# Attention's norms brought to the features' partitions by block transposes and DRAM instead of TensorE transposes

## Chip, cores and metric

The kernel runs on one core of one Trainium2 chip. The metric is the device time of one execution in microseconds (us). A core has TensorE (PE in the profile: matmuls, and transposes as matmuls against an identity; PEld is its weight load), VectorE (DVE), ScalarE (ACT), GpSimd (POOL) and SyncE (SP), which here only issues DMAs. Each engine works through its own instructions in order, and waits for the others by semaphores. SBUF is the memory on the chip, with 128 partitions; PSUM holds what TensorE writes; DRAM lies outside.

## What is computed

Four sequences of 512 tokens with 256 features go through a gated-scan attention and then six FFN blocks, all in f32:

```python
# x: (4, 512, 256)
x = x + layernorm(attn(layernorm(x)))
x = x + layernorm(ffn(layernorm(x)))

# attn(x), hidden sizes 128 and 512
q = silu(x @ Wq1 @ Wq2);  f = sigmoid(x @ Wk1 @ Wk2);  v = x @ Wv
a = sigmoid(f)                          # exp(log_sigmoid(f))
h[t] = a[t] * h[t - 1] + (1 - a[t]) * v[t]      # along the tokens
out = q * h
attn = (out * rsqrt(mean(out * out) + 1e-6) * norm_w) @ Wo

# ffn(x): six blocks, hidden size 1024
for i in range(6):
    x = gelu(x @ W1[i].T + B1[i]) @ W2[i].T + B2[i] + x
    if i < 5: x = layernorm(x) * LN_G[i] + LN_B[i]
```

Each sequence has two norms in front of matmuls that concern this case: the *first norm*, ahead of the attention, and the *second norm*, ahead of the FFN. A layernorm is taken over the features of one token, so it is done with tokens on the partitions; the matmuls that follow sum over features, so they want features on the partitions. Between the two the data has to be transposed.

## The kernel before

**Layout.** A sequence's x lies as four tiles of 128 tokens by 256 features (`xs[b][t]`). `token_stats` (L658) and `rstd_of` (L668) make a norm's mean and reciprocal deviation on DVE and POOL, and `normalized` (L682) applies them on ACT into a tile of the ring `nns` (named n in the profile).

**To the features, first way.** `to_features` (L699) takes the four normalized tiles and, for each half d of the features, lets TensorE transpose four blocks of 128x128 into one PSUM tile (`pt`), which ACT copies to SBUF (128x512). Attention's first norms (`Attention.features`, L774, and `first_features`, L779) and second norms (`ffn_input`, L896) go this way.

**To the features, second way.** `passage` (L733) takes the same tiles through DRAM. DVE transposes every 32x32 block in two instructions of 128x512 (`blocks_transposed`, L712); SP stores the result to a DRAM tile of the ring `passed` (512 KB); `collected` (L722) reads it back in four DMAs of 128 KB, each to 32 partitions, so that blocks come to lie in the right partitions; then ACT copies each half d while it puts the columns in order (four tiles by four groups by 32 columns). The norms between FFN blocks go this way (`Norm.norm`, L1148, and `Norm.features`, L1191), where that last copy also applies the scale and the bias. A passage takes two buffers of `rooms` (the four x tiles, and two `room` tiles that attention's output projection uses), gives one back at once and the other after the copies.

**Order of work.** The Python code only records operations, with a cost and with the buffers that they read and write, slice by slice. `Plan.run` (L302) then simulates the engines and writes out each engine's instructions: of those that can start it takes the one that is due first (`Plan.latest`, L285: backward from the end of TensorE's work). So a change in one place moves instructions elsewhere. The semaphores are put in afterwards from what each instruction reads and writes. All stores and nearly all loads are issued by SP, in that written order.

**Stages.** Sequences go through attention one after another (the loop at L1235). While sequence b is in its projections and scans, the first norm of b+1 is prepared, the output projection of b-1 is done (`output`, L853; `residual`, L868, which makes x1 = x + layernorm(attention) and the statistics of the second norm), and the second norm of b-2 is brought to the features (`ffn_input`). Each scan takes sigmoids on ACT, the scan on DVE, and products and sums on POOL. The FFN works on two sequences at a time (g = 0 is sequences 0 and 1): `input_sums` (L649) makes 18 sums of input blocks (`tx`, B_SUMS) on POOL, `w1_sums` 19 sums of weight blocks (`sa`), and `Hidden` multiplies these and the plain blocks, in a scheme with fewer products; `Output` does the second matmul. The second norms of sequences 2 and 3 come to the features while the FFN's first half (i = 0, g = 0) runs; this is ordered by class `Attended` (L1208).

Buffers that matter: `txs` are 18 tiles of 128x256; the first four serve as features of sequence 0, and the last as the source of warm-up matmuls; the others lie idle until the first `input_sums`. `xts[g][d][n]` hold the features that enter the FFN (xt in the profile), `tcs` the features of attention (tc).

Of the kernel before, what the change touches and what calls it, by code (L numbers as in the profile page):

```python
# [12 lines left out]
AF = mybir.ActivationFunctionType  # L13
# [3 lines left out]
P = 128  # L17
# [123 lines left out]
def lines_of(text):  # L141
    return [line.split() for line in text.strip().split("\n")]
# [205 lines left out]
def kernel(  # L348
# [46 lines left out]
    def tiles(name, shape, n=1, pool=sb):  # L395
        return [
            Buf(pool.tile(shape, F32, tag=f"{name}{k}", name=f"{name}_{k}"))
            for k in range(n)
        ]
# [39 lines left out]
    w2_s = tile_of("w2", [P, NH, E])  # L439
    sa = tiles("sa", [P, 2 * P], len(lines_of(A_SUMS)))  # L440
    sb2 = tiles("sb", [P, NP, P], 4)
    txs = tiles("tx", [P, 2 * P], len(lines_of(B_SUMS)))

    wide = Pool(tiles("tmp", [P, S], 14))

# [12 lines left out]
        [View((v, *xs[b]), v.ap, (0,) * (NT + 1)) for b, v in enumerate(x_of)]  # L458
        + [View((v, *ys.bufs[2 * k : 2 * k + 2]), v.ap, (0,) * 3) for k, v in enumerate(roomy)]
    )  # L460
    passed = Ring(tiles("passed", [P, NT * E], 4, dram))
    banks = Pool(tiles("bank", [P, S], 6, ps))
    pts = Ring(tiles("pt", [P, S], 2, ps))
    sts = Ring(tiles("st", [P, 6], 6))
# [5 lines left out]
    def act(dst, src, func=AF.Copy, bias=None, scale=None):  # L470
        given = [(k, p) for k, p in (("bias", bias), ("scale", scale)) if p is not None]
        ptrs = [p for _, p in given if isinstance(p, View)]
        kw = {k: p.ap if isinstance(p, View) else p for k, p in given}
        plan.op(
            "ACT",
            0.054 + 0.00084 * src.size + 0.11 * len(ptrs),
            lambda: nc.scalar.activation(dst.ap, src.ap, func, **kw)  # L477
            if func != AF.Copy
            else nc.scalar.copy(dst.ap, src.ap),  # L479
            [src, *ptrs],  # L480
            [dst],
        )
# [153 lines left out]
    def x_blocks(g):  # L636

        blocks = {
            f"b{k}{c}": xts[g][k][c // 2][:, ts(c % 2, 2 * P)]
            for k in range(ND)  # L640
            for c in range(4)
        }
        blocks.update((f"t{n}", t) for n, t in enumerate(txs))
        return blocks

    def w1_sums(i):
# [35 lines left out]
    def normalized(src, by, t):  # L682

        r, nb = by
        z = nns.next()
        to = z
        if len(src.ap.shape) == 3:
            to = z.with_ap(z.ap.rearrange("p (f r) -> p f r", r=src.ap.shape[2]))
        act(to, src, AF.Identity, nb[:, t : t + 1], r[:, t : t + 1])
        return z  # L690
# [8 lines left out]
    def to_features(srcs, d, xt, scale=None, bias=None):  # L699


        pt = pts.next()[:, : len(srcs) * P]
        for t, src in enumerate(srcs):
            transpose(pt[:, ts(t, P)], src[:, ts(d, P)])
        if scale is None:
            act(xt, pt)
        else:
            act(xt, pt, AF.Identity, bias, scale)
# [21 lines left out]

        plan.op("SP", 0.45 * Q, emit, [there], [to], to.size * P * 4 / 0.26e6)

    def passage(tokens):  # L733

        block, there, to = rooms.next(), passed.next(), rooms.next()
        by_pair = block.with_ap(block.ap.rearrange("p (f t c) -> p f t c", t=NT, c=32))
        for k in range(0, NT, 2):
            z = tokens[k : k + 2]  # L740
            pair = pairs[id(z[0].bufs[0])].rearrange("p (t f r) -> p f t r", t=2, r=32)
            blocks_transposed(by_pair[:, :, k : k + 2, :], pair, *z)
        store(there, block)
        collected(there, to)
        rooms.back(block)
        return to

    class Attention:

# [4 lines left out]
        def norm(self):  # L754
            self.n, mv = [], mvs.next()
            for t in range(NT):
                token_stats(mv, xs[self.b][t], t)
            by = rstd_of(mv, rs.next())
            for t in range(NT):
                self.n.append(normalized(xs[self.b][t], by, t))  # L760
            self.xt = []

        def first_norm(self):
            self.n = []
# [8 lines left out]

        def features(self, d):  # L774
            xt = tcs.next()
            to_features(self.n, d, xt)
            self.xt.append([xt])

        def first_features(self, half):  # L779

# [87 lines left out]
        def residual(self):  # L868
# [24 lines left out]
                store(kept[self.b][t], x1)  # L893
            self.x1_by = rstd_of(mv1, rs.next())

        def ffn_input(self, d):  # L896

            if d == 0:
                self.n1 = [normalized(xs[self.b][t], self.x1_by, t) for t in range(NT)]
            g, n = divmod(self.b, 2)  # L900
            to_features(self.n1, d, xts[g][d][n])

    class Row:

# [236 lines left out]
    class Norm:  # L1141
# [6 lines left out]
        def norm(self, n):  # L1148

            room, mv = self.output.tokens[n], mvs.next()  # L1150
            by_tile = room.ap.rearrange("p (f t r) -> p t f r", t=NT, r=32)
            y = [room.with_ap(by_tile[:, t]) for t in range(NT)]
            for t in range(NT):
                token_stats(mv, y[t], t)
            by, tokens = rstd_of(mv, rs.next()), []
            for t in range(NT):
                z = normalized(y[t], by, t)
                tokens.append(z)
                if self.i == NB - 1:
                    b = 2 * self.g + n  # L1160
                    tt("POOL", z, z, self.x[n][:, ts(t, E)], ALU.add)
                    store(out[b, ts(t, P), :], z)
            rooms.back(room)
            if self.i < NB - 1:
                self.there[n] = passage(tokens)
            else:
                rooms.back(self.x[n])

# [22 lines left out]
        def features(self, u):  # L1191
            if self.i == NB - 1:
                return
            n, d = divmod(u, ND)
            src, dst = self.there[n][:, ts(d, S)], xts[self.g][d][n]
            act(
                dst.with_ap(dst.ap.rearrange("p (t g c) -> p g t c", t=NT, g=Q)),
                src.with_ap(src.ap.rearrange("p (g t c) -> p g t c", t=NT, g=Q)),
                AF.Identity,
                be_s[:, self.i, d : d + 1],  # L1200
                g_s[:, self.i, d : d + 1],
            )
            if d == ND - 1:
                rooms.back(self.there[n])
            if u == 2 * ND - 1:
                input_sums(self.g)

    class Attended:  # L1208
# [8 lines left out]
        def norm(self, u):  # L1217
            if u == 0:
                self.both[1].residual()

        def features(self, u):
            n, d = divmod(u, ND)
# [12 lines left out]
    for b in range(B):  # L1235
        one = att[b]
        past = att[b - 1] if b else None
        one.k1_q1()
        if b == 0:
            for _ in range(FILL):  # L1240
                plan.op("PE", 0.43, lambda: warm(P), [one.n[1]], [unread])
        if b + 1 < B:
            att[b + 1].norm()
        one.value(0)
        one.scan(0)
        one.value(1)
        if past:
            past.output(0)
        one.scan(1)
        if past:  # L1250
            past.output(1)
        one.value(2)
        if past:
            past.output(2)
        one.scan(2)
        if past:
            past.output(3)
        one.value(3)
        if past:
            past.residual()  # L1260
        if b >= 2:
            att[b - 2].ffn_input(0)
        if b + 1 < B:
            att[b + 1].features(0)
        one.scan(3)
        if b >= 2:
            att[b - 2].ffn_input(1)
        if b + 1 < B:
            att[b + 1].features(1)
# [3 lines left out]
    w2_sums()  # L1273

    output, norm = None, Attended(att[2], att[3])
    for i in range(NB):
        for g in range(NG):
            last, hidden = output, Hidden(i, g)
            if last:
                hidden.take(HEAD)  # L1280
                while last.left:
                    last.take(BY[0])
                    hidden.take(BY[1])
                norm = Norm(*of, last)
            else:
                hidden.take(4)
            if g == 0:
                if i:
                    load_w2(i)
                    w2_sums()  # L1290
                if i + 1 < NB:
                    load_w1(i + 1)
            if last:
                for n in range(2):
                    hidden.take(2)
                    if of[0] == NB - 1:
                        norm.load_x(n)
                    norm.norm(n)
            else:
                for u in range(4):  # L1300
                    hidden.take(2)
                    norm.tokens(u)
                norm.norm(0)
            hidden.take(26)
            if g == 1 and i + 1 < NB:
                w1_sums(i + 1)
            output = Output(i, g, hidden)
            for u in range(4):
                output.take(2)
                norm.features(u)  # L1310
            output.take(len(output.left) - DEFER)
            of = (i, g)
# [57 lines left out]
```

## Time and profile before

| | |
|---|---|
| times of three runs | 693.93, 694.00, 694.45 us (median 694.0) |
| profiled execution | 694.03 us, of which the profile's span is 691.4 us |
| granted TensorE clock, mean | 0.996 |
| transposes of `to_features` on PE | 64, between 6.2 and 145.3 us |
| attention, by PE's first and last instruction of it | about 6 to 123 us |
| DVE block transposes | 84, all between 144 and 636 us |
| DMA | 67.4 MB in 74,444 packets, mean 98 GB/s |

The span is what the profiler covers; the execution's time has some 2.6 us around it. In the profile's group rows, "x64 | 10.1, 283 | 0.0" says: 64 instructions, 10.1 us busy in all, 283 ns mean of one, and the idle time of the engine just before them with what ended it. An f32 matmul of the kernel shows as two matmul records, a transpose as one. The view of waits lists per engine: who waited for whom, us in total, times, longest. Timeline rows give the start, the length, the engine, the line and what was written from what, with equal neighbours merged. Here are the engines' shares of the attention and the first FFN half, from the view by windows (us busy):

| window | PE | DVE | ACT | POOL | DMA share |
|---|---|---|---|---|---|
| 15 to 45 | 30.0 | 16.4 | 20.2 | 28.5 | 0.24 |
| 45 to 75 | 30.0 | 19.7 | 20.0 | 22.0 | 0.06 |
| 75 to 105 | 30.0 | 14.7 | 19.5 | 20.7 | 0.05 |
| 105 to 135 | 29.6 | 19.9 | 21.4 | 27.1 | 0.20 |
| 135 to 165 | 30.0 | 14.9 | 11.9 | 22.4 | 0.09 |

### The profile page before, as it was taken

The page shows a single profiled execution, that of the slowest core. Times are in us where ns is not written, and L with a number is a line of the kernel's source. Part 1 is how long each engine was busy: PE and PEld are TensorE (multiplying, and loading weights), DVE is VectorE, ACT ScalarE, POOL GpSimd, SP SyncE. Part 2 cuts the span into 40 slices and gives each one's busy share as a digit, 9 for nine tenths or more (in the row PEclk, how much of TensorE's full clock was granted, in tenths as well). Part 3 has the DMA queues.
Part 4 walks back from the last instruction along what each step waited for, and adds up shares of the span by engine and source line. Part 5 has one row for each costly group of instructions (what it writes and reads, how often), then busy time and mean ns, then how long its engine had stood idle before and what let it go on. Part 6 is the DMA issues. An engine that isn't in the chain of part 4 may idle for free.

```text
span 691.4 us, 8158 instructions
## 1 busy us (share of the span) xinstructions
PE 677.8 (98%) x2376; PEld 440.9 (64%) x2376; DVE 460.2 (67%) x885; ACT 358.2 (52%) x625; POOL 528.6 (76%) x688
## 2 busy tenths in 40 slices
PE   9999999999999999999999999999999999999994
PEld 7565568856747658568476475584674765855853
DVE  5566455745956948839659569487495694793955
ACT  3847756842724635536447346354473482463732
POOL 4997659694978758986679887589866798865862
PEclk9999999999999999999999999999999999999998
DMA  8300002102254042351341541414514305316411
GB/s 252 100 1 31 27 4 90 33 16 89 79 153 152 31 148 66 148 169 48 119 126 63 167 136 46 150 49 166 169 30 148 96 1 194 110 61 182 138 46 62
DMA packets 74444, 67.43 MB, mean 98 GB/s; under 512 B 5792, under 2 KB 64160, under 8 KB 74400
## 3 DMA queue, kind: packets, MB, share of 16 engines
q1 hardware_dynamic: 73568, 65.99, 29.8%
q10 hardware_dynamic: 832, 0.92, 0.4%
q8 instruction: 19, 0.31, 0.2%
q14 instruction: 25, 0.20, 0.1%
HBM read 40.68 MB, written 26.21 MB: 97 GB/s over the span
## 4 chain that ended last, share of the span: by engine, by line
PE 71%; DVE 14%; POOL 6%; ACT 4%; issue 3%; DMA 1%; DVEq 0%; ACTq 0%; POOLq 0%
PE bank L526 66%; DVE ht L494 8%; POOL tc L494 5%; PE pt L526 4%; DVE tmp L494 2%; DVE st L663 2%; ACT ht L477 2%; ACT tmp L479 1%; PE pt L537 1%; DVE tc L494 1%; POOL r L494 1%; DMA xt<-in_wk 1%; DVE mv L664 1%; POOL r L506 1%; ACT n L477 1%
## 5 line engine op out<-in xcount | busy, mean ns | idle before, releaser
L526 PE MATMUL bank<-tx,sa 128*128 128x256 f32 x672 | 163.4, 380 | 2.2 <-ACT tmp L479 2.2
L479 ACT COPY tmp<-bank 128x512 f32<-128x512 f32 x144 | 83.6, 583 | 145.5 <-PE bank L526 136.5
L526 PEld LDWEIGHTS bank<-tx,sa 128*128 128x128 f32 x672 | 126.2, 190 | 30.8 <-issue 10.9
L494 POOL TENSOR_TENSOR tc<-ht,tc 128x512 f32<-128x512 f32 x96 | 123.8, 1302 | 21.2 <-ACT bank L477 20.5
L477 ACT ACTIVATE ht<-ht,b 128x512 f32<-128x512 f32 x156 | 106.9, 715 | 14.8 <-DVE ht L494 14.7
L494 DVE TENSOR_TENSOR ht<-tmp,bank 128x512 f32<-128x512 f32 x156 | 101.5, 677 | 18.3 <-ACT tmp L479 14.7
L526 PE MATMUL bank<-tc,w 128*128 128x512 f32 x208 | 95.0, 592 | 0.0
L494 DVE TENSOR_TENSOR tmp<-tmp,bank 128x512 f32<-128x512 f32 x96 | 64.2, 677 | 42.3 <-PE bank L526 24.5
L516 DVE SCALAR_TENSOR_TENSOR tmp<-bank,b,xt 128x512 f32<-128x512 f32 x48 | 35.6, 742 | 84.8 <-PE bank L526 84.8
L526 PE MATMUL bank<-tc,sb 128*128 128x512 f32 (+1 forms) x200 | 88.7, 580 | 1.4 <-POOL tc L494 0.6
L526 PE MATMUL bank<-ht,sb 128*128 128x512 f32 (+1 forms) x200 | 88.4, 576 | 0.0
L526 PE MATMUL bank<-ht,w 128*128 128x512 f32 x192 | 84.7, 592 | 0.0
L494 POOL TENSOR_TENSOR tx<-xt,tx 128x256 f32<-128x256 f32 x108 | 75.7, 726 | 0.9
L526 PEld LDWEIGHTS bank<-tc,sb 128*128 128x128 f32 x200 | 37.0, 190 | 48.3 <-issue 36.8
L477 ACT ACTIVATE n<-x,r 128x256 f32<-128x256 f32 x88 | 46.9, 587 | 36.1 <-POOL r L494 35.9
L526 PEld LDWEIGHTS bank<-tc,w 128*128 128x128 f32 x208 | 39.1, 190 | 40.5 <-issue 38.5
L526 PEld LDWEIGHTS bank<-ht,w 128*128 128x128 f32 x192 | 36.3, 190 | 39.8 <-issue 34.4
L526 PEld LDWEIGHTS bank<-ht,sb 128*128 128x128 f32 x200 | 37.8, 190 | 34.8 <-issue 31.8
L494 POOL TENSOR_TENSOR tx<-xt 128x256 f32<-128x256 f32 x24 | 17.4, 727 | 53.6 <-ACT xt L477 53.5
L526 PE MATMUL bank<-tx,w 128*128 128x256 f32 x224 | 56.8, 379 | 0.0
L494 DVE TENSOR_TENSOR tmp<-bank,tmp 128x512 f32<-128x512 f32 (+1 forms) x54 | 35.9, 665 | 27.6 <-PE bank L526 26.0
L526 PE MATMUL bank<-xt,w 128*128 128x256 f32 x192 | 50.9, 379 | 0.0
(80 smaller groups left out, 1011.4 us busy)
## 6 DMA issues: line engine op xcount, KB each, us to landing
x<-passed SPq DMA_DIRECT2D x116, 128.0 KB, 2.9
passed<-x SPq DMA_DIRECT2D x30, 256.0 KB, 2.2
room<-passed SPq DMA_DIRECT2D x52, 128.0 KB, 3.1
w<-in_w1t SPq DMA_DIRECT2D x6, 1024.0 KB, 5.0
w<-in_w2t SPq DMA_DIRECT2D x6, 1024.0 KB, 5.8
passed<-x SPq DMA_DIRECT2D x12, 512.0 KB, 2.7
passed<-room SPq DMA_DIRECT2D x8, 512.0 KB, 2.8
passed<-room SPq DMA_DIRECT2D x14, 256.0 KB, 2.2
```

The lines of the kernel that those rows point to most:

```text
L477: lambda: nc.scalar.activation(dst.ap, src.ap, func, **kw)
L479: else nc.scalar.copy(dst.ap, src.ap),
L494: lambda: on(engine).tensor_tensor(dst.ap, a.ap, b.ap, alu),
L506: lambda: on(engine).tensor_scalar(dst.ap, src.ap, *by, op0, **kw),
L516: lambda: nc.vector.scalar_tensor_tensor(dst.ap, a.ap, by, b.ap, op0, op1),
L526: lambda: nc.tensor.matmul(dst.ap, lhs.ap, rhs.ap, start=start, stop=True, skip_group_check=True),
L537: lambda: nc.tensor.transpose(dst.ap, src.ap, ident.ap),
L663: nc.vector.bn_stats(st.ap, src.ap)
L664: nc.vector.bn_aggr(mv.ap[:, t, :], st.ap)
```

## The change

The first norms of sequences 2 and 3 and the second norms of all four sequences take the second way, `passage`, instead of `to_features`. The first norms of sequences 0 and 1 stay with TensorE. For this:

- `passage` is given the pool from which it takes its two buffers. In attention this is a new pool `early` of three buffers laid over `txs[4]` to `txs[15]`, which are made as one tile `tx` of 18 slices so that four neighbours form one buffer of 128x1024. The second norms of sequences 2 and 3 use `rooms`.
- The ring of DRAM tiles `passed` grows from four to eight.
- The ordering copy on ACT becomes a helper `in_order`, without scale and bias for attention's norms.
- The second norm is normalized in a new step `ffn_norm`, recorded ahead of the two `ffn_input` steps that only copy. In the loop it stands after `att[b + 1].norm()`, for sequence 2 ahead of the FFN loop, and for sequence 3 in `Attended.norm`.

```diff
-    txs = tiles("tx", [P, 2 * P], len(lines_of(B_SUMS)))
+    tx_of = tile_of("tx", [P, len(lines_of(B_SUMS)) * 2 * P])
+    txs = [Buf(tx_of.ap[:, ts(k, 2 * P)]) for k in range(len(lines_of(B_SUMS)))]
...
+    early = Pool(
+        [
+            View(tuple(txs[k : k + NT]), tx_of.ap[:, k * E : (k + NT) * E], (0,) * NT)
+            for k in range(NT, 4 * NT, NT)
+        ]
+    )
+    passed = Ring(tiles("passed", [P, NT * E], 8, dram))
-    passed = Ring(tiles("passed", [P, NT * E], 4, dram))
...
-    def passage(tokens):
+    def passage(tokens, rooms):
...
+    def in_order(xt, there, d, *by):
+
+        src = there[:, ts(d, S)]
+        act(
+            xt.with_ap(xt.ap.rearrange("p (t g c) -> p g t c", t=NT, g=Q)),
+            src.with_ap(src.ap.rearrange("p (g t c) -> p g t c", t=NT, g=Q)),
+            *by,
+        )
...
             for t in range(NT):
                 self.n.append(normalized(xs[self.b][t], by, t))
             self.xt = []
+            if self.b > 1:
+                self.there = passage(self.n, early)
...
         def features(self, d):
             xt = tcs.next()
-            to_features(self.n, d, xt)
             self.xt.append([xt])
+            if self.b == 1:
+                to_features(self.n, d, xt)
+                return
+            in_order(xt, self.there, d)
+            if d == ND - 1:
+                early.back(self.there)
...
+        def ffn_norm(self, rooms):
+            n1 = [normalized(xs[self.b][t], self.x1_by, t) for t in range(NT)]
+            self.rooms, self.there = rooms, passage(n1, rooms)
+
         def ffn_input(self, d):
 
-            if d == 0:
-                self.n1 = [normalized(xs[self.b][t], self.x1_by, t) for t in range(NT)]
             g, n = divmod(self.b, 2)
-            to_features(self.n1, d, xts[g][d][n])
+            in_order(xts[g][d][n], self.there, d)
+            if d == ND - 1:
+                self.rooms.back(self.there)
...
             if u == 0:
                 self.both[1].residual()
+                self.both[1].ffn_norm(rooms)
...
         if b + 1 < B:
             att[b + 1].norm()
+        if b >= 2:
+            att[b - 2].ffn_norm(early)
...
     output, norm = None, Attended(att[2], att[3])
+    att[2].ffn_norm(rooms)
```

The norms between FFN blocks keep their passages; their copy now goes through `in_order` with the same scale and bias, and they pass `rooms`.

## What is predicted

> **What bounds the kernel now.** I read the page's first two parts, then the waits of PE (TensorE's matmuls), then PE in order of time.
>
> ```profile
> PE 677.8 (98%) x2376; PEld 440.9 (64%) x2376; DVE 460.2 (67%) x885; ACT 358.2 (52%) x625; POOL 528.6 (76%) x688
> PEclk9999999999999999999999999999999999999998
> ```
>
> PE is busy for 98% of the span at full clock, and no other engine passes 76%.
>
> ```profile
> PE bank L526 <- ACT tmp L479: 2.2, 6, 0.4
> PE bank L573 <- DVE ones L581: 1.2, 1, 1.2
> PE bank L526 <- POOL tc L494: 0.6, 1, 0.6
> ```
>
> All waits of PE make 4.0 us. So an instruction taken off PE shortens the kernel, until a wait takes its place. The transposes that go stand in PE's timeline like this (start, length, group):
>
> ```profile
> 49.08 0.95 PE L526 MATMUL pt<-ones,ht 128*128 128x1 f32 x8
> 49.89 0.64 PE L537 MATMUL pt<-ident,n 128*128 128x128 f32 x4
> 50.37 1.88 PE L526 MATMUL bank<-tc,w 128*128 128x512 f32 x4
> 52.08 0.60 PE L537 MATMUL pt<-ident,n 128*128 128x128 f32 x4
> 52.52 3.60 PE L526 MATMUL bank<-tc,xt 128*128 128x512 f32 x8
> ```
>
> Four transposes hold back the next product by 0.44 to 0.48 us (50.37 - 49.89, 52.52 - 52.08). The same view gives PE's pace: an f32 product of 512 columns is two records and takes 0.86 us, one of 256 columns 0.43 us.
>
> **What goes.** `to_features` loses the first norms of sequences 2 and 3 and all four second norms: 6 x 2 x 4 = 48 of 64 transposes. From starts in the timeline their eleven stretches cost 0.92 (near 50 us), 1.78 (75.7 to 79.2), 0.91 (102 to 105) and 1.74 us (137.6 to 145.4): **5.35 us**, 0.11 us each. The group's row says something else:
>
> ```profile
> L537 PE MATMUL pt<-ident,n 128*128 128x128 f32 x64 | 10.1, 283 | 0.0
> ```
>
> By its mean, 48 x 0.283 would be 13.6 us. The Trainium skill (Perfetto Trace Analysis, Identifying the Most-Contended Engine) says that matmul busy time misjudges PE because matmuls are pipelined; the starts are 0.11 us apart under records of 0.28, so I take 5.35. A second rule speaks against the change: VectorE: DVE Perf Modes, Rules for kernel authors, sends a 128x128 transpose to TensorE where a PSUM destination will do, and The three transpose paths puts it at 390 ns there (bf16) against 311 ns for VectorE's, which only turns 32x32 blocks. By 390 ns the removal would be worth 48 x 0.39 = 18.7 us; the trace's 0.11 decides. What the rule weighs is one transpose against another; here PE is the bound and DVE idles a third of the span, so the question is only whether the detour arrives in time.
>
> **What comes.** Six passages: each two DVE block transposes, one 512 KB store, four 128 KB loads, then two ACT copies from SBUF in place of two from PSUM. The kernel already does this in the FFN, so rows exist:
>
> ```profile
> L717 DVE STREAM_TRANSPOSE x<-n 128x512 f32<-128x512 f32 x24 | 16.2, 688 | 0.4 <-ACT n L477 0.4
> x<-passed SPq DMA_DIRECT2D x116, 128.0 KB, 2.9
> passed<-x SPq DMA_DIRECT2D x12, 512.0 KB, 2.7
> ```
>
> - DVE: 12 x 0.69 = 8.3 us more. From 15 to 150 us it is busy for 81 of 135 us; it has room. The harm is order: transposes stand ahead of scans.
> - ACT: the old copies take 0.58 us. No SBUF copy with regrouped columns is in the trace. Nearest are the square of ht (SBUF, plain, 0.63) and the FFN's regrouped xt with scale and bias (0.81). So 12 x 0.05 to 0.23 = 0.6 to 2.7 us, beside PE; I take 0.7 each. [...]
> - SP: 6 x (0.33 + 4 x 0.61) = 16.6 us of issues on a queue that is nearly empty before 145 us, and 6.3 MB in slices where the page shows 0 to 2 tenths of DMA use.
> - Latency, from the last DVE block: store landed after 2.7, issues 0.61 apart so the last starts 1.8 later, landing 3.0 more, handovers 0.2: 7.7 us, then the copy.
> - The larger ring `passed` and the one tile for `tx` issue nothing. Buffers are tracked slice by slice, so I cost them at 0; were `tx` treated whole, each product on tx would wait for later sums at 0.73 us of POOL each, which the written order of waits doesn't show.
>
> **Arrival against need.** I walked the order that the planner writes for the changed kernel, with the durations above; PE's times are those of before less what is removed.
> - Sequence 2, first norm: blocks done about 27 (behind the third scan, which was at 24.7), landed 36 (the store also waits for the weight loads ahead), needed 52.5 - 0.9 = 51.6. Hidden.
> - Sequence 3, first norm: need is 79.2 - 0.92 - 1.78 + 0.43 (one output product is moved ahead of it) = 76.9. Its four normalizations (0.5 each) now stand between the two sigmoids of a scan, right after the first, at 63.6 to 65.6; the blocks end at 66.2, landed 74.0. ACT comes to the copies only behind the square of ht that was at 76.0 and now ends at 75.7 (DVE's extra blocks cost the scan before it 0.5): copied 76.4 and 77.1, for products at 76.9 and 77.8. Slack 0.5 us. The delayed scan (1.5 us) holds a PSUM bank that PE asks for 5 us later. Behind the copies on ACT: the sigmoids of the sequence's last scan.
> - Second norm of sequence 0: its store stands behind that passage on SP, landed 80, copied 83, used by POOL's sums at once and by PE only at 102. Hidden.
> - Second norm of sequence 1: POOL puts two sums of tx and two of ht before the end of its rstd, which is ready at 89.1; normalized by 91.2, blocks done 93.0 behind a token_stats, landed 101. ACT is at its last sigmoids until 102.6, the copy ends 103.3. Need: column sums at 101.55 - 2.7 = 98.85, then products of 0.8, 1.7, 0.9 and 1.3 us: 103.5. Slack 0.2. Behind this copy ACT has bank copies and normalizations to do; one product waits about 0.4 us for its bank.
> - Sequence 2, second norm: stored at 141.6, but its loads wait on SP behind a store of the first FFN output (until 144.4); landed 149.3, needed 152.9.
> - Sequence 3, second norm: the first half's products end at 135.9 - 3.6 = 132.3. From there DVE's last combinations and token_stats (to 137.1), two GELUs (to 140.1), two POOL sums of 1.27 with the rstd between (to 143.1), four normalizations (145.2), the blocks (146.0); the store waits for sequence 2's loads to be issued (147.2), landed 155.4, copied 156.1. Need: 29 products of 0.86 us after 132.3, 157.2. Slack 1.1. Behind: ACT's bank copies, and POOL's sums (0.73 each), which stay ahead of products of 0.86.
>
> From the second half of the first FFN block on, PE's order is the same in both kernels, so what is gained there is carried to the end.
>
> **Sum.** Profiled execution 694.03 (span 691.4 and 2.6 around it; median shown 694.0). Less 5.35 is 688.7. New waits: 0.4 at the banks, and 0.5 for three slacks of 0.2 to 1.1 us that my walk doesn't know better than to a microsecond. The waits that were there (0.4 from an ACT copy in each block, 0.6 from POOL) stay. **689.6 us.**
>
> **Rivals.**
> 1. Late passages (slower). For: SP issues in order, two passages stand in series before sequence 3's features, and three slacks are about nothing. The trace shows loads whose issue took 1.2 instead of 0.61 us (+2.4 a passage) and landings of 4.8 against 3.3 (+1.5). If that falls on the chain of sequences 2 and 3 it is 2.4 + 3.9 - 1.1 = 5.2 us of stall, and 3.9 - 1.6 = 2.3 on sequence 1, whose loads land 1.6 before ACT is free: 688.7 + 7.5 = 696.2. It turns to slower from 5.35 us of stall. Against: those are extremes of rows taken in the loaded FFN; here DMA is nearly idle. Chance 0.08; about another 0.06 for stalls near 5 us that leave no change.
> 2. DVE and ACT order delays the scans: the 1.5 us shows up on PE once or twice: 691 us. For: in-order queues. Against: PE asks for those banks 5 us later. 0.2.
> 3. More than removed: the stalls near 120 and 160 us (0.4 to 0.7 each by the starts) vanish with the freed PSUM buffers: 688.0. Against: they are ACT's table load and bank copies. 0.1.
> 4. The change doesn't do what it says: excluded by the written order, which has 48 transposes fewer and 12 block transposes more.
> The forecast itself has 0.56.
>
> **Range and chances.** 688.0 takes in rival 3, 692.4 rival 2 and half of the stalls of rival 1 (+3.7): about 8 in 10. Three runs of before lie within 0.5 us, so 0.2%, 1.4 us, can be told. Faster 0.86 (forecast, 2, 3), same 0.06, slower 0.08.
>
> **What would show it.** 16 transposes on PE; k1 of sequence 3 near 76.9; PE's waits on ACT xt and tc copies under 1 us in all; the first stretch of tx products without a gap. Wrong if ACT waits for DMA into tx or x for microseconds and PE's gaps before 160 us add up to more than 5.

## The result, and the profile after

The changed kernel takes **687.25 us** (median of 4 runs, 686.87 to 687.62) against 694.14 us before (4 runs, 693.93 to 694.45): a ratio of 0.990 with a 95% interval of 0.989 to 0.992. It is faster by 6.9 us where 4.4 were predicted, and lies 0.75 us below the range. Its profiled execution took 687.01 us with a span of 685.2, so 6.2 us went from the span and 0.8 from what lies around it (2.6 before, 1.8 after).

The busy row and the clock row of the page after:

```profile
PE 671.6 (98%) x2328; PEld 436.1 (64%) x2328; DVE 469.2 (68%) x897; ACT 358.0 (52%) x625; POOL 529.1 (77%) x688
PEclk9999999999999999999999999999999999999998
```

PE still bounds the kernel at full clock: 48 instructions and 6.2 us fewer, as much as the span lost. DVE, with twelve block transposes more, is busy 9 us longer. All waits of PE after:

```profile
PE bank L534 <- ACT tmp L487: 1.5, 4, 0.4
PE bank L581 <- DVE ones L589: 1.2, 1, 1.2
PE pt L545 <- DVE n L514: 0.6, 1, 0.6
PE pt L545 <- ACT tx L487: 0.2, 1, 0.2
PE bank L534 <- DMA xt<-in_wk: 0.2, 1, 0.2
```

No wait on a copy of the new passages (ACT xt or tc) is among them. The two on pt are at the first transposes, before 8 us, which the change leaves as they are. Two of the six waits on an ACT copy are gone (126.3 and 175.2 us in the timeline before; the expectations below call the first "near 123"), and the wait on POOL tc (192.5). The forecast has all of them stay. PE in order of time near 50 us, where k1 is the product of the normalized x with Wk1, the first to use the new features:

```profile
49.08 0.95 PE L534 MATMUL pt<-ones,ht 128*128 128x1 f32 x8
49.89 1.96 PE L534 MATMUL bank<-tc,w 128*128 128x512 f32 x4
51.69 3.60 PE L534 MATMUL bank<-tc,xt 128*128 128x512 f32 x8
```

The column sums start at the same 49.08 us as before, the eight transposes behind them are gone, and k1 of sequence 2 starts 0.83 us earlier (52.52 before), 0.10 for each. At the tightest place that the prediction named, k1 of sequence 3, PE and then ACT:

```profile
76.66 0.60 PE L534 MATMUL pt<-xt,ht 128*128 128x256 f32 x2
77.09 3.60 PE L534 MATMUL bank<-tc,xt 128*128 128x512 f32 x8
```

```profile
75.09 0.63 ACT L485 ACTIVATE ht<-ht 128x512 f32<-128x512 f32 x1 [2.19 <-POOL ht L502]
75.63 1.12 ACT L487 COPY tc<-tx 128x512 f32<-128x512 f32 x2
```

The copies stand behind the square of ht and end at 76.75, the product starts at 77.09 with no wait in brackets. Two copies from SBUF take 1.12 in a row, the second starting before the first has ended. The passages' DMA rows, and one of DVE's (these blocks write to x; there were 24 before. Into room they are 12 where 16 were, and 8 new ones write to tx: twelve more in all):

```profile
passed<-tx SPq DMA_DIRECT2D x4, 512.0 KB, 2.6
tx<-passed SPq DMA_DIRECT2D x16, 128.0 KB, 3.0
```

```profile
L725 DVE STREAM_TRANSPOSE x<-n 128x512 f32<-128x512 f32 x32 | 21.7, 689 | 0.9 <-ACT n L485 0.9
```

**Where the gain sits.** The table gives the start of the same PE instruction in each kernel less its start before (in us, negative is earlier); both are counted from k1 of sequence 1, since the first loads shift everything by up to 0.7 us from one execution to the next. The last two columns are experiments told below.

| place on PE (start before) | after | second norms only | old order, no transposes | work put back |
|---|---|---|---|---|
| k1 of sequence 2 (52.5) | -0.83 | 0.00 | -0.83 | 0.00 |
| column sums of sequence 2 (101.6) | -2.54 | -0.88 | -1.35 | 0.00 |
| column sums of sequence 3 (122.3) | -3.37 | -1.71 | -1.95 | -0.01 |
| first FFN block, end of half 1 (135.9) | -4.02 | -2.23 | -1.94 | -0.66 |
| end of half 2 (184.8) | -6.08 | -3.65 | -3.69 | -0.96 |
| first block's output (232.2) | -6.60 | -4.42 | -3.70 | -1.45 |
| last transposes on PE (681.3) | -6.20 | -4.38 | -3.05 | 0.13 |

After has gained 3.37 by 122 us, where 32 transposes have gone: 0.105 each. Between 122 and 136 no transpose goes and 0.65 is gained; 16 transposes and 0.3 more go until 185; 0.5 until 192. Near 446 us the profiled execution gives 0.4 back, and `work_back` gives 0.4 and 1.1 back in late blocks; the last section comes back to this.

### The profile page after: what moved, and what is told of

It is laid out like the page before. It is cut to its first block, busy times and chain, and to the rows that moved or that the text cites. A ratio compares the mean times of both kernels' runs of the same rounds, so it can differ in the third digit from the quotient of the medians.

```text
span 685.2 us, 8143 instructions
## 1 busy us (share of the span) xinstructions
PE 671.6 (98%) x2328; PEld 436.1 (64%) x2328; DVE 469.2 (68%) x897; ACT 358.0 (52%) x625; POOL 529.1 (77%) x688
## 4 chain that ended last, share of the span: by engine, by line
PE 64%; DVE 16%; POOL 8%; ACT 4%; issue 3%; DMA 2%; SPq 0%; DVEq 0%; ACTq 0%; POOLq 0%
PE bank L534 60%; DVE ht L502 9%; POOL tc L502 5%; PE pt L534 4%; DVE tmp L502 2%; DVE st L671 2%; ACT ht L485 2%; DVE tc L502 1%; POOL tx L502 1%; POOL r L502 1%; ACT tmp L487 1%; DMA passed<-room 1%; DMA xt<-in_wk 1%; DVE mv L672 1%; POOL r L514 1%
## 5 line engine op out<-in xcount | busy, mean ns | idle before, releaser
L485 ACT ACTIVATE n<-x,r 128x256 f32<-128x256 f32 x96 | 50.4, 581 | 37.4 <-POOL r L502 37.4
L502 POOL TENSOR_TENSOR tx<-xt 128x256 f32<-128x256 f32 x24 | 17.5, 727 | 60.1 <-ACT xt L485 50.9
```

The source lines that it names most:

```text
L502: lambda: on(engine).tensor_tensor(dst.ap, a.ap, b.ap, alu),
```

## Experiments

Each was timed in 3 to 5 rounds beside the kernel before, whose median was 694.1 to 694.2 with single runs from 693.1 to 694.9.

**1. The parts by themselves.** In `first_norms` the second norms go through PE again, in `second_norms` the first norms do, in `storage` both:

```diff
 first_norms, storage: ffn_input(d)
-            in_order(xts[g][d][n], self.there, d)
+            to_features(self.n1, d, xts[g][d][n])
 second_norms, storage: features(d)
-            in_order(xt, self.there, d)
+            to_features(self.n, d, xt)
```

> Only the first norms of sequences 2 and 3 take the passage; the four second norms go back to transposes (16 of 64 transposes gone). If each part brings what its transposes cost and the old waits go only with the new order of work at the start of the FFN: 0.83 + 0.84 = 1.7 us less, so 692.4, with PE's waits on ACT near 123 and 172 us and on POOL near 190 us still there. If the freed PSUM buffers remove those waits: up to 1 us more, 691.4. If the 0.8 us outside the span belongs to the passages and not to their number: another 0.8 less.

> Only the four second norms take the passage (32 of 64 transposes gone). Transposes alone: 3.4 us less, 690.7. If the old waits near 123, 160 to 172 and 190 us go with them: 1.5 us more, 689.2. With first_norms alone the two gains should add up to the 6.9 us of the whole change; if they add up to clearly less, the gain is one of the order of work and not of the parts.

> Only the storage is changed: the sums of the FFN input in one tile, the DRAM ring of 8, and no passage beyond those of before. The prediction: nothing, 694.1 within 0.3, 2.6 us outside the span. If the time outside the span comes from how many tiles are declared: 693.3, with 1.8 outside. If one tile makes products wait for sums of other slices: 695 or more.

Measured: first norms 692.19 (ratio 0.9968, 0.9956 to 0.9980), second norms 688.48 (0.992, 0.991 to 0.993), storage 693.78 (0.9998, 0.9990 to 1.0005). So storage costs nothing, as predicted. The waits of PE with the first norms only, and then with the second norms only:

```profile
PE bank L534 <- ACT tmp L487: 2.2, 6, 0.4
...
PE bank L534 <- POOL tc L502: 0.9, 3, 0.6
```

```profile
PE bank L534 <- ACT tmp L487: 1.5, 4, 0.4
```

With the first norms only, the old waits are all there; with the second norms only they are gone, and PE ends 4.4 us earlier (column "second norms only" of the table) for 3.4 us of transposes. The gains, 2.0 and 5.7, add up to 7.7; the 0.8 around the span came in both (1.8 us in each), so counted once they make the 6.9 of the change.

**2. What a transpose costs.** The kernel before, with the 48 transposes done twice:

```diff
+        for t, src in enumerate(srcs * (times - 1)):
+            transpose(pt[:, ts(t, P)], src[:, ts(d, P)], 0.0)
```

> The kernel before with the same 48 transposes done twice each, the second time at a price of nothing for the planner, all else in the order of before. By the spacing of the starts (0.11 us each): 694.1 + 5.2 = 699.3. By the mean of the group's row (0.283): 707.7. By the page's 390 ns: 712.8. If waits hide some of them, less than 699.3.

(The last of these is an estimate from the 390 ns that the prediction cites from VectorE: DVE Perf Modes, The three transpose paths.)

Measured: 699.22 us (ratio 1.0071, 1.0055 to 1.0086), and 5.26 later on PE at its end: 0.110 each. The group's row of that kernel still shows records of 277 ns:

```profile
L537 PE MATMUL pt<-ident,n 128*128 128x128 f32 x112 | 15.3, 277 | 0.0
```

The prediction's 0.11 by the spacing of the starts is confirmed, and 5.35 for the 48 is right within 0.2.

**3. The transposes taken away, the order kept.**

```diff
+                plan.op("PE", 0.107, lambda: None, [src], [pt])   (in place of each transpose)
-        act(xt, pt)
+        act(xt, pair)                                             (two of the four normalized tokens)
```

> The kernel before without the 48 transposes and without any passage: the copies take the normalized tokens as they stand, so the turning of the features is left out. The planner still reckons with the transposes, so every engine's order is that of before, and the copies still wait their turn for the PSUM buffer. If the old waits of PE go only with a new order of work: 694.1 less 5.1 = 689.0, waits on ACT near 120 and 170 us and on POOL near 185 us still there. If taking the transposes off PSUM and PE removes those waits by itself: 687.5 or less. 0.8 less in either case if the time outside the span follows the transposes.

Measured: 691.04 us (0.9953, 0.9941 to 0.9966), only 3.1 less than before. All the old waits are there, and new ones came. PE and then ACT of this kernel near k1 of sequence 3:

```profile
77.81 4.03 PE L526 MATMUL bank<-tc,xt 128*128 128x512 f32 x8 [0.56 <-ACT tc L479]
```

```profile
76.16 0.60 ACT L479 COPY xt<-n 128x512 f32<-128x512 f32 x1
76.67 0.59 ACT L477 ACTIVATE tmp<-bank 128x512 f32<-128x512 f32 x1
77.16 0.61 ACT L479 COPY tc<-n 128x512 f32<-128x512 f32 x1
```

PE asks for it earlier than before, but ACT makes the copy for k1 only third in its old order, and PE waits 0.56 (0.8 by the starts) and 0.4 more behind it. So 1.4 of the 5.1 us turned into waits by 185 us. (Another 0.6 goes near 392 us; see the end.)

**4. The order kept, the work put back.** Both are the change with PE's transposes added, unread. First with the transposes of the tokens as operations of the planner (`put_back`), then without the planner's knowledge (`work_back`), four transposes of the identity inside the operation of the product that opens a bank:

```diff
 work_back
+        def emit():
+            for _ in range(turns):
+                nc.tensor.transpose(dst.ap[:, :P], ident.ap, ident.ap)
+            nc.tensor.matmul(...)
```

> The change with the 48 transposes put back beside the passages, at a price of nothing for the planner: they turn the same tokens into PSUM and nobody reads the result, so the order of the other engines stays that of the change. If the order removed the old waits: 687.2 + 5.1 = 692.3 with none of them back. If the freed PSUM buffers and PE slots did: 694 with the waits back.

> The change with PE's work of the 48 transposes put back and the order of every engine kept to the instruction: four transposes of the identity stand ahead of each of twelve products that open a bank, near the places of the old ones, and the product then overwrites them. If the old waits of PE (ACT near 123, POOL near 190 us) went with the written order, they stay away: 687.25 + 48 x 0.107 = 692.4. If they went because PE has less to do and so the other engines' results come at another time, they are back: 693.3 to 693.9.

Measured: `put_back` 693.28 us (0.9987, 0.9981 to 0.9994), `work_back` 692.76 (0.9981, 0.9975 to 0.9988). In `put_back` the wait near 126 us stayed away, but those near 175 (0.3) and 192 us (0.6) were back. It was no clean test: contrary to what its expectation says, the planner had written the engines in another order than the change's, DVE from 67 us on, POOL from 114, ACT from 125 and PE from 130. In `work_back` the order of every engine is that of the change to the instruction. Of PE's five waits in it, these are on ACT and POOL:

```profile
PE bank L540 <- ACT tmp L487: 1.5, 4, 0.4
PE bank L540 <- POOL tx L502: 0.8, 1, 0.8
PE bank L540 <- POOL tc L502: 0.2, 1, 0.2
```

The four on ACT copies are those of after, and the two on POOL are at 475 and 490 us, in a late block: near 126, 175 and 192 us PE does not wait. With all of PE's old work in place the new order alone is 1.45 us ahead of the kernel before by 232 us (last column of the table); the whole change is 6.60 ahead, and 6.60 - 1.45 = 5.15 is the transposes. In `old_order` PE's work is gone and the waits stay; here it is there and they are gone. So they went with what the planner writes anew for the engines, not with the work that PE lost. (This is the order together with the other engines' changed work, such as copies from SBUF in place of PSUM; the experiments don't part these two.)

**5. Whose order?** `old_pe_order` is the change with PE's products in the order of before in four places of the first FFN block; `new_pe_order` is the kernel before with three of these places in the order of the change. Only the sequence of PE is edited.

```diff
+        for first, own in SWAPS:
+            for k, m in enumerate(own):
+                pe[where[first + k]] = prods[m]
```

> The change with PE's products written in the order of before in four places of the first FFN block (15 products near 110 to 125 us, three small swaps in the second half), all else as in the change. If the order on PE removed the old waits: they come back, 0.65 near 123 and some 0.8 near 170 to 190 us, 688.7. If the order of ACT, DVE and POOL did: 687.25, no wait back.

> The kernel before, all 64 transposes in place, with only the three small swaps of PE's products in the second half of the first FFN block taken from the change. If PE's order there removes the wait on POOL near 190 us: 694.1 less 0.5 to 0.8, 693.4. If it takes the other engines' order or the missing transposes: 694.1.

Measured: 692.79 us (0.9982, 0.9975 to 0.9988) and 694.22 (1.0004, 0.9996 to 1.0012). In the second half PE's order is not the cause: its old order under the other engines' new one brings no old wait back, and its new order in the kernel before removes none (POOL tc still 0.7). There ACT, DVE and POOL decide; whose of the three was not tried. In the first half the old order of PE costs 5.5 us, by a new wait of 3.7 and by the clock, which is halved from 106.8 to 110.3 us (some 1.7 us more). PE of `old_pe_order`:

```profile
105.85 1.14 PE L564 MATMUL bank<-tx,sa 128*128 128x256 f32 x4 [3.70 <-POOL tx L532]
106.81 1.88 PE L564 MATMUL bank<-xt,sa 128*128 128x256 f32 x4
```

A product on tx stands ahead of output products that could have run, and POOL has its sum 3.7 us later. Since PE then came late to the place near 126 us, this run does not tell whose order removed the wait there. The timelines do. The kernel before, then the change:

```profile
124.63 1.08 ACT L477 ACTIVATE n<-x,r 128x256 f32<-128x256 f32 x2
125.61 0.56 ACT L479 COPY tmp<-bank 128x512 f32<-128x512 f32 x1
126.32 1.97 PE L526 MATMUL bank<-tx,sa 128*128 128x256 f32 x8 [0.42 <-ACT tmp L479]
```

```profile
119.58 0.72 ACT L485 ACTIVATE ht<-ht,b 128x512 f32<-128x512 f32 x1
120.85 0.58 ACT L487 COPY tmp<-bank 128x512 f32<-128x512 f32 x1 [0.54 <-PE bank L534]
```

Before, two normalizations of sequence 2's second norm, 1.0 us, stand on ACT right ahead of the copy that empties the bank PE asks for, and ACT has had no idle time since its table load at 119.4 us. In the change the planner puts these normalizations at 132.3 us and the table load 3.4 us earlier, counted from the column sums of sequence 3; ACT is idle for 0.54 until PE has filled the bank, and PE does not wait. `old_order` and `first_norms`, which have this wait, have the two normalizations there; `put_back`, `work_back` and `old_pe_order`, which don't, have them later. So it is ACT's order that removed this wait; which of the two moves was enough was not tried. The two other old waits come to PE through a late result of DVE (near 175) and through POOL's sums (near 192), and no single instruction was found for them.

**6. How much room the passages have.** Each gets a copy from DRAM to DRAM between store and loads:

```diff
         store(there, block)
+        for _ in range(trips - 1):
+            far = passed.next()
+            plan.op("SP", 0.0, lambda a=far, b=there: nc.sync.dma_start(out=a.ap, in_=b.ap), [there], [far])
+            there = far
         collected(there, to)
```

> The change with a copy from DRAM to DRAM put into each of the six passages (its place in the order of the queue is right behind the store; the order of all other work is kept): each arrives some 2.5 to 3 us later. By the prediction's slacks (0.5 us for sequence 3's first norm, 0.2 and 1.6 before ACT for sequence 1's second, 1.1 for sequence 3's second) 2.5 + 1.2 + 1.9 = 5.6 us of stall on PE: 692.9. If the slacks were really larger, as the absence of any wait in the change's trace suggests (about 0.9, 1.9 and 1.6): 2.1 + 1.1 + 1.4 = 4.6, 691.8. If the passages have several microseconds of room: 687.5.

Measured: 705.75 us (1.0163, 1.0145 to 1.0181), far worse than any theory gave. The copy took 4.0 us, not 2.5 to 3. ACT of this kernel, and PE:

```profile
87.69 1.14 ACT L487 COPY xt<-tx 128x512 f32<-128x512 f32 x2 [4.32 <-DMA tx<-passed]
```

```profile
78.50 3.70 PE L534 MATMUL bank<-tc,xt 128*128 128x512 f32 x8 [1.83 <-ACT tc L487]
...
110.80 2.07 PE L534 MATMUL bank<-xt,sa 128*128 128x256 f32 x4 [5.32 <-ACT xt L487]
```

At k1 of sequence 3 four microseconds of delay cost 2.0 by the starts, so there were about 2.0 of room. But the copy of sequence 0's second norm, which PE needs only 20 us later, makes ACT stand still for 4.3 us, and everything behind it on ACT is late with it, the norm that feeds the next passage too. That passage, sequence 1's second norm, starts 5.3 us late besides its own 4.0 (counted from k1 of sequence 1), and PE waits 5.5 by the starts; near 170 us the same again, 5.7. The rest, 4.3 us, is the clock. The granted TensorE clock is the column behind POOL's; around the first of these waits:

```profile
107.00:108.00 1.00, 0.00 (x0) 0.00 (x0) 0.96 (x3) 0.00 (x0) 0.00 (x0) 0.83 0.69 201
113.00:114.00 1.00, 1.00 (x4) 0.73 (x4) 0.00 (x0) 0.99 (x2) 1.00 (x2) 0.50 0.00 0
114.00:115.00 1.00, 1.00 (x5) 0.86 (x4) 0.00 (x0) 0.00 (x0) 1.00 (x2) 0.76 0.00 0
```

PE stops at 105.3 by the starts. A mean of 0.83 between 107 and 108 puts the halving at 107.7, 2.4 us later; 0.76 between 114 and 115 puts the return at 114.5, after 3.7 us of work at half clock (4.5 at the second wait). The sum on PE: 2.0 + (5.5 + 1.9) + (5.7 + 2.3) = 17.4 of the 17.5 us by which this kernel is behind the change at 185 us.

**7. One norm more.** The first norm of sequence 1 by the passage too:

```diff
-            if self.b > 1:
+            if self.b:
                 self.there = passage(self.n, early)
```

> The change, and sequence 1's first norm takes the passage too (56 of 64 transposes gone). If it arrives in time: 0.9 us less than the change, 686.4. It has only some 6 us from the norm to the first product: the passage took 9 us from the last block transpose to the copy for sequence 2. So it is likely late by some 3 to 6 us, and the planner puts sequence 0's output products ahead of it, which may fill part of this: 686.4 to 691; I expect 689.

Measured: 691.79 us (0.9963, 0.9950 to 0.9976), worse than the change by 4.5. k1 of sequence 1 starts 7.1 us later than before; the output products of sequence 0 that the planner puts ahead of it fill 3.4 of this and themselves wait 2.2 us for POOL, 0.7 and 1.5. At the end of the second stop the clock is halved, too, from 31.9 to 35.3 us, which costs some 1.7 us:

```profile
31.98 2.08 PE L534 MATMUL pt<-xt,ht 128*128 128x256 f32 x4 [1.45 <-POOL ht L502]
```

```profile
33.00:34.00 1.00, 1.00 (x4) 0.82 (x3) 0.09 (x1) 0.88 (x3) 1.00 (x2) 0.50 0.70 175
```

No version tried beats the change.

## Why the prediction was wrong

The direction and the main term, the transposes' price, were right. Two small terms failed, in the same direction: new waits, put at 0.9 us, did not come, and old waits, put at unchanged, went (1.45 us). Another 0.8 us lies outside the span and stood in no term.

- **What goes**: 5.35 us by the spacing of the starts. Right: 5.15 (experiment 4), against 13.6 by the records' length and the estimate of 18.7 from the page's 390 ns.
- **What comes**: DVE's blocks took 0.68 to 0.71 each (0.69), the SBUF copies 0.60 to 0.63 (0.7 assumed), the passage of sequence 1's second norm 7.7 us from the last block to the landing (7.7). All hidden, as said.
- **Arrival against need**: at the three tight places the walk was good to a microsecond. First norm of sequence 3 copied 75.6 to 76.8 (76.4 and 77.1 predicted), needed 77.1 (76.9); second norm of sequence 1 copied 103.45 (103.3), needed 103.8 (103.5); second norm of sequence 3 copied 155.2 (156.1), needed 156.8 (157.2). None made PE wait.
- **"New waits: 0.4 at the banks, and 0.5 for three slacks"**: failed, 0.9 us that did not come. Slacks of 0.2 to 1.1 with an error of a microsecond were priced as a small loss. In the trace they are 0.9, 0.3 and 1.6 from the copy to the need, so which side the error fell on was partly luck. Rival 2, scans delayed by the new order of DVE and ACT, did not show either: none of PE's waits is on a scan.
- **"The waits that were there stay"**: the step that failed most, 1.45 us. It rested on "From the second half of the first FFN block on, PE's order is the same", which was false by three swaps. But the swaps did not do it (experiment 5): what I had not compared past the first half was the order of ACT, DVE and POOL, which had changed there too. In the first half the forecast put the wait at 126 us down to ACT's table load and bank copies, and did not ask whether the change moves what stands ahead of them on ACT. It does: the table load and two normalizations (experiment 5).
- **Rival 3**, more than removed, was the case, with the wrong reason: freed PSUM buffers. In experiment 3 no transpose takes a buffer or PE's time, and the waits stay.
- **The 2.6 us around the span** were taken as fixed; 1.8 after. No step had this 0.8.
- **Rival 1**, late passages, did not happen, but its price was mis-sized: 7.5 us of stall for delays of 2.4 and 3.9. A delay of 4.0 cost 17.5, since a late copy holds ACT for all behind it and the stopped PE comes back at half clock. The rival had no term for the clock, though the Trainium skill (TensorE: Matmul & The Clock Gate, What's actually happening) has the rule: an idle window of about 3.4 us halves it, until about 3.4 us of work. The 3.4 to 4.5 us of work at half clock agree roughly. What starts it does not: in `two_trips` the halving came 2.4 us after PE stopped, and in `seq1_too` behind stops of 0.7 and 1.5 us, which by the rule would cost no clock and cost some 1.7 us. So in this case shorter stops are enough; how short, the runs don't tell.

In sum: 689.6 - 0.9 - 1.45 - 0.8 and 0.2 back for the transposes is 686.65; the 0.4 near 446 us makes 687.05, where the profiled execution took 687.01.

## What to carry to other kernels

Where a planner writes the order of the instructions, a change that takes work away also writes a new order for every engine: compare that order on all engines for as far as it differs, and test it by putting the work back inside existing operations, which parts the two effects (here 5.15 and 1.45 us). Take what a pipelined engine spends on an instruction from the spacing of starts, not from the records' length. A detour that is hidden by two microseconds is hidden only while nothing is queued in order behind its last wait: price a late arrival by what stands behind the waiting copy and by the clock of the engine that stops.

## What the runs showed of the hardware besides

- The time around the span belongs to the program as built: 2.55 to 2.68 us in 48 runs of before, the same for `storage` and `twice`, 1.74 to 1.87 in every run of the kernels with passages in the attention, 2.2 to 2.4 for `old_order` and `new_pe_order`, which have none. It follows neither the transposes (`put_back` has all of them and 1.8) nor the passages alone; what sets it stays open.
- Single executions of one kernel differ by 2.4 us in `put_back` (691.9 to 694.4), and by 3.7 in `seq1_too` (690.1 at a mean granted clock of 0.996, 693.8 at 0.991), where the slowest run has the lowest clock and the fastest the highest. Two other sources show in the profiled executions: the first loads shift k1 of sequence 1 between 26.1 and 27.3 us, and in some executions PE waits 0.3 to 0.8 us in a later FFN block for a sum on POOL behind a passage's loads (0.3 near 392 us in `old_order`, 0.7 near 395 in `old_pe_order`, 0.8 near 490 in `work_back` and `put_back`). The 0.4 that the change gives back near 446 us shows no wait of PE. How often these come in each kernel the profiles, one of each, don't tell; so the medians of `work_back` and the change lie 5.5 apart where the traces give 5.15.
